# Cross keys by seven block products, exponentials straight from PSUM, and block sums of the gate weights made at loading, in a decoder layer

## The chip, the cores and the metric

The kernel runs on one core of one Trainium2 chip, in float32. A core has five engines that run side by side, each with its own in-order queue: TensorE (matrix products into PSUM; in the profile PE, and PEld for its weight loads), VectorE (DVE), ScalarE (ACT), GpSimd (POOL) and SyncE (SP), from which most DMAs are issued. The metric is device time in microseconds. Before the change the median of three runs is 1415.14 us (1413.28 to 1415.62). The profiled execution took 1413.7 us, of which its span is 1411.5.

## The reference, cut to what matters

The program is one pre-norm decoder layer on 16 sequences of 112 tokens with width 512 and 16 heads of 32: self-attention, cross-attention on a context of 375 rows with a mask, and a gated feed-forward layer with a Walsh-Hadamard transform. What the change touches:

```python
# cross-attention
k = _nan_clean(proj(at, Wk, bk, T))          # 16 batches of 375 context rows
scores = jnp.einsum('bhsd,bhtd->bhst', q, k) / scale
scores = jnp.clip(scores, -50.0, 50.0)
scores = jnp.where(attend, scores, -10000.0)
scores = jnp.clip(scores, -50.0, 50.0)
probs = jax.nn.softmax(scores, axis=-1)
...
# feed-forward
up_gate = jnp.einsum('bsd,hd->bsh', x, W1)
up_lin = jnp.einsum('bsd,hd->bsh', x, W3)
hidden = jax.nn.silu(up_gate) * up_lin
```

A masked score is -50 after the second clip, so its exponential is exp(-50).

## The kernel before, in words

`finite_layer` computes the layer under the assumption that all values are finite and within limits, and collects statistics (`seen`) on the way. Near the end they become one flag, `unfit`; `decoder_layer` reads it and runs the careful `general_layer` if it is set. All times here are of runs without it.

TensorE's order is written out by hand (line 1497, `manual_schedule`): its instructions run in the order of the source. The instructions of the other engines are ordered by a planner, which takes what it expects to be ready, earlier source lines first; `issue_after` holds instructions behind a named one. Each engine then runs its queue in order on the chip.

Stages: self-attention of 16 batches (`lay`, line 1525), cross-attention of 16 batches in three steps each (lines 1572 to 1609), then two feed-forward passes of half the tokens (lines 1636 to 1694).

`Filler` holds generators of independent work. Each `yield` carries a planned cost in microseconds; `fill(us)` draws pieces until that much is spent, with over- or underspending carried on, and `drain` runs the rest. So what TensorE does between two attention steps is fixed by the planned costs. In the cross stage batch `b` is attended while keys, values and queries of `b + 1` are made as filler: with 20.5 us planned for keys and values, 6.0 for queries (made for two batches at every odd `b`), 13.0 for the projection of a finished group of batches at `b` = 0, 4 and 8, and 2.0 for its transposes at `b` = 2, 6 and 10; a third goes to each step.

One cross step (`Cross.step`, line 1128) takes one of three blocks of 125 context rows: 16 score products fill two PSUM tiles `sc` of two banks each; VectorE clips each to SBUF (line 1141), with the upper limit per row from the mask (`hi`); ScalarE takes the exponential in place (line 1144). On TensorE the weighted values of the step before follow (`weigh`, line 921), after a third step its key sums too (line 932), then filler. VectorE adds the exponentials of the three blocks (line 1164) and, in `Pending.store`, takes the reciprocal of the sums (line 951) and multiplies (line 952).

`Keys.keys` runs `features` (line 846): for each of four column groups, four products of 375 columns into one `mm` bank, then an eviction with bias on ScalarE (line 859). There are two `mm` banks, in turn, shared with all filler. `squares` (line 864) has VectorE put the sums of squares of keys and queries into `seen`. `Keys.values` makes value rows per block (line 883; evicted on line 888).

The feed-forward pass computes each pair of 128-column blocks of W1 and of W3 by seven products of half-size blocks (`Pass.products`, line 1337), which needs four sums of weight blocks. They are made in the cross stage, in batches 1 to 9: `weight_sums` (line 1198) loads the raw blocks, adds them on VectorE behind the clip (line 1218), and stores 1 MB tiles to DRAM; `load_blocks` (line 1222) reads these back, one for each of 16 tiles of a pass. All 1 MB weight tiles share eight buffers (tag `w`); normalised tiles and other rows share four (tag `row`).

## Time and profile before

| what | value |
|---|---|
| median of three runs | 1415.14 us |
| profiled execution | 1413.7 us, span 1411.5 us |
| TensorE busy | 1383.3 us (98%) |
| VectorE busy | 790.0 us (56%) |
| ScalarE busy | 365.3 us (26%) |
| cross stage, about 340 to 855 us | TensorE 509.3, VectorE 326.6, ScalarE 162.9 of 515 us |
| DMA | 115.89 MB, mean 82 GB/s |

A row of groups gives line, engine, operation, output<-inputs, shapes and count, then busy time, mean ns of one, and the idle time of the engine just ahead of these instructions with what ended it. A float32 product of the source is two MATMUL records. Busy time of overlapping records is counted once, so a group's busy time divided by its count can be less than its mean. The chain is the work that ended last, followed back; its lines give start, length and line, with the count of instructions.

### The profile page before, as it was taken

The numbers are of one execution on the slowest core, as the hardware profiler recorded it, in microseconds if no ns is written. First come the engines' busy times: TensorE is split into PE (matmuls) and PEld (weight loads), VectorE is DVE, ScalarE is ACT, GpSimd is POOL, SyncE is SP. The second block draws the span as 40 slices with busy tenths as digits, with TensorE's granted clock in tenths as the row PEclk, the third lists the DMA queues.
The fourth block names the chain that finished last, engine by engine and source line by source line (L and its number), as shares of the span: only waits on it lengthen the run. The fifth ranks groups of instructions, "written<-read, shape, count | busy, mean of one in ns | idle before, by whom it ended". The sixth has DMA issues, their size and how long they took to land.

```text
span 1411.5 us, 19018 instructions
## 1 busy us (share of the span) xinstructions
PE 1383.3 (98%) x8096; PEld 764.8 (54%) x8096; DVE 790.0 (56%) x1340; ACT 365.3 (26%) x561; POOL 30.7 (2%) x46
## 2 busy tenths in 40 slices
PE   8999999999999999999999999999999999999997
PEld 5555555556565646564656655554555555555553
DVE  5146987676566586558665547745644224444332
ACT  3245352324133323331333333111110001111000
POOL 2000010101001000000000000000000000000000
PEclk9999999999999999999999999999999999999999
DMA  8100002611123324322020010223022223521301
GB/s 313 47 1 23 8 16 75 243 56 44 38 100 132 113 91 133 112 83 82 23 82 23 23 61 31 92 88 118 30 94 85 90 97 122 191 90 63 116 0 54
DMA packets 49729, 115.89 MB, mean 82 GB/s; under 512 B 2896, under 2 KB 31584, under 8 KB 41188
## 3 DMA queue, kind: packets, MB, share of 16 engines
q1 hardware_dynamic: 47968, 111.39, 22.3%
q0 software_dynamic: 672, 1.62, 0.4%
q10 hardware_dynamic: 996, 1.59, 0.3%
q8 instruction: 65, 1.06, 0.3%
q14 instruction: 28, 0.23, 0.0%
HBM read 86.80 MB, written 27.79 MB: 81 GB/s over the span
## 4 chain that ended last, share of the span: by engine, by line
PE 90%; DVE 6%; DMA 1%; ACT 1%; issue 1%; ACTq 0%; POOLq 0%
PE mm L851 21%; PE mm L883 13%; PE gate L1351 12%; PE mm L894 7%; PE ys L1351 7%; PE gate L1287 6%; PE mm L1351 5%; PE sc L910 4%; PE ys L921 4%; PE ys L1287 3%; PE mm L1287 3%; PE ys L932 2%; PE sc L1017 1%; DMA cT<-in_ctx 1%; PE mm L1435 1%; PE mm L812 1%
## 5 line engine op out<-in xcount | busy, mean ns | idle before, releaser
L883 PE MATMUL mm<-xv,cT 128*125 128x512 f32 x384 | 173.3, 598 | 1.8 <-ACT v L888 1.8
L851 PE MATMUL mm<-cT,xk 128*128 128x375 f32 x512 | 167.5, 483 | 3.5 <-DMA cT<-in_ctx 2.2
L851 PEld LDWEIGHTS mm<-cT,xk 128*128 128x128 f32 x512 | 95.3, 190 | 73.5 <-issue 11.1
L883 PEld LDWEIGHTS mm<-xv,cT 128*125 128x125 f32 x384 | 70.0, 188 | 81.3 <-issue 73.7
L1351 PE MATMUL gate<-t,f 128*128 128x448 f32 x256 | 101.4, 539 | 0.0
L1141 DVE TENSOR_SCALAR e<-sc,hi 125x896 f32<-125x896 f32 x64 | 70.8, 1144 | 48.6 <-PE sc L910 48.6
L951 DVE RECIPROCAL r<-ys 128x448 f32<-128x448 f32 x32 | 94.3, 2947 | 2.8 <-PE ys L932 2.8
L1144 ACT ACTIVATE e<-e 125x896 f32<-125x896 f32 x64 | 60.9, 952 | 115.5 <-DVE e L1141 82.7
L1287 PE MATMUL gate<-h,f 128*128 128x448 f32 x224 | 86.6, 539 | 0.0
L998 DVE TENSOR_REDUCE mx<-sc 112x8 f32<-112x896 f32 x32 | 33.5, 1085 | 87.3 <-PE sc L910 87.3
L1351 PE MATMUL gate<-xyT,f 128*128 128x448 f32 x192 | 80.1, 540 | 0.0
L1351 PE MATMUL ys<-t,f 128*128 128x448 f32 x192 | 77.4, 539 | 0.0
L1351 PEld LDWEIGHTS gate<-t,f 128*128 128x128 f32 x256 | 48.6, 190 | 47.6 <-issue 47.2
L867 DVE CUSTOM_DVE_ANT_0 junk<-kT 128x375 f32<-128x375 f32 x64 | 34.2, 534 | 64.1 <-ACT kT L859 64.1
L1164 DVE TENSOR_TENSOR es<-es,e 125x896 f32<-125x896 f32 x64 | 68.6, 1090 | 0.4
L1141 DVE TENSOR_SCALAR es<-sc,hi 125x896 f32<-125x896 f32 x32 | 36.6, 1147 | 52.1 <-PE sc L910 45.4
L1287 PEld LDWEIGHTS gate<-h,f 128*128 128x128 f32 x224 | 42.5, 190 | 41.3 <-issue 40.9
L888 ACT COPY v<-mm 125x512 f32<-125x512 f32 (+1 forms) x64 | 37.0, 580 | 105.2 <-PE mm L883 105.1
L910 PEld LDWEIGHTS sc<-q,kT 32*125 32x125 f32 x1536 | 46.2, 183 | 31.9 <-issue 19.8
L859 ACT ACTIVATE kT<-mm,bk 128x375 f32<-128x375 f32 x64 | 36.5, 572 | 89.9 <-PE mm L851 89.9
L883 PE MATMUL mm<-wv,xyT 128*112 128x512 f32 x128 | 57.8, 596 | 0.3 <-ACT v L888 0.3
L1367 ACT COPY u<-gate 128x448 f32<-128x448 f32 x16 | 8.5, 532 | 186.2 <-PE gate L1351 163.3
(179 smaller groups left out, 1940.0 us busy)
## 6 DMA issues: line engine op xcount, KB each, us to landing
f<-blocks SPq DMA_DIRECT2D x46, 1024.0 KB, 4.8
blocks<-o SPq DMA_DIRECT2D x16, 1024.0 KB, 5.4
cT<-in_ctx SPq DMA_DIRECT2D x16, 750.0 KB, 4.9
o<-in_f_w SPq DMA_DIRECT2D x32, 256.0 KB, 3.7
w<-in_f_w SPq DMA_DIRECT2D x4, 1024.0 KB, 9.2
blocks<-w SPq DMA_DIRECT2D x4, 1024.0 KB, 6.5
xr<-in_x SPq DMA_DIRECT2D x2, 1024.0 KB, 10.5
out_y<-o SPq DMA_DIRECT2D x8, 256.0 KB, 4.8
```

The lines of the kernel that those rows point to most:

```text
L851: nc.tensor.matmul(acc[:, :n], w[:, c, ts(j, P)], src[:, c, :], start=(c == 0), stop=(c == C - 1))
L883: nc.tensor.matmul(acc[:n, :], src[:, c, :], w[:, c, :], start=(c == 0), stop=(c == C - 1))
L888: nc.scalar.copy(dst[:n].rearrange("p h r -> p (h r)"), acc[:n, :])
L894: nc.tensor.matmul(acc, xyT[:, c, ts(t, P)], w[:, c, :], start=(c == 0), stop=(c == C - 1))
L910: nc.tensor.matmul(views[i // 2][:, i % 2, j, :], k_of(i, j), q_of(i, j), start=True, stop=True)
L921: nc.tensor.matmul(y[ts(i, DH), j, :], v[:, HG * j + i, :], es[i // 2][:n, i % 2, j, :], start=first and j == 0, stop=last, skip_group_che ...
L951: nc.vector.reciprocal(r, sums)
L1141: self.clip = nc.vector.tensor_scalar(e[:KP], sc, -CLIP, hi[:, n : n + 1], op0=ALU.max, op1=ALU.min).ins
L1144: nc.scalar.activation(e[:KP], e[:KP], AF.Exp, scale=SCALE)
L1164: nc.vector.tensor_tensor(total, total, late[3][i][:KP], ALU.add)
L1287: nc.tensor.matmul(banks[m][bank], o[:, c, ts(m, P)], t[:, c, :], start=first and c == 0, stop=c == UNITS - 1, skip_group_check=True,)
L1351: nc.tensor.matmul(bank, o[:, s, k, :], t[:, k, :], start=first and k == 0, stop=k == 1, skip_group_check=True,)
```

## The change

1. **Keys.** `Keys.keys` no longer calls `features`. The 512 x 512 weight and the 512 x 376 context block (a column of zeros is added by a GpSimd memset) are cut into 2 x 2 blocks, and seven products of half-size blocks take the place of eight. Four sums of weight blocks (`xks`) are made once; four sums of context blocks (`t_sums`) for each batch, at the start of the batch before. A product is 4 matmuls of 188 columns into one bank (`a`, `b` and `d`, from the two `mm` buffers); ScalarE evicts bank `a` twice with the bias, VectorE adds the others up into the key tile. Each product yields a planned 1.28 us.
2. **Exponentials.** VectorE's clip goes. ScalarE reads the scores from PSUM with a scale per row (0 for masked rows) and a bias per row (-50 for masked rows). The lower limit is checked by a Relu over the scores, in place in PSUM, with its sum into `low`; the upper limit by a Relu on the reciprocals of the sums, into `top`. Both must be zero in the end, or the flag is set. The reciprocal is taken in two halves. The four ScalarE passes come ahead of the weighted values in the source.
3. **Statistics.** `squares` goes, for keys and queries.
4. **Gate weights.** `weight_sums` and its tiles in DRAM go. `load_blocks` loads the two raw halves and has VectorE make the four sums in the loaded tile.
5. **Order.** The filler takes the first two value blocks, then keys, then the third; keys and values are planned at 19.5 us (from 20.5), the first keys at 9 (from 12.5). The raw mask now uses a `row` buffer.

```diff
+    zero = keep.tile([P, 2 * B * KC + B], F32, name="zero")
+    nc.gpsimd.memset(zero, 0.0)
+    low, top = zero[:, : 2 * B * KC], zero[:, 2 * B * KC :]
...
-    mi = keep.tile([KP, B * KC], I32, name="mi")
+    mi = row("mi").bitcast(I32)[:KP, : B * KC]
     nc.gpsimd.dma_start(out=mi, in_=mask_t)
...
+    nc.gpsimd.tensor_scalar(scl, mi, 0.5, SCALE, op0=ALU.is_gt, op1=ALU.mult)
+    nc.gpsimd.tensor_scalar(nscl, scl, -1.0, None, op0=ALU.mult)
+    nc.gpsimd.tensor_scalar(bia, mi, 0.5, 50.0, op0=ALU.is_gt, op1=ALU.mult)
+    nc.gpsimd.tensor_scalar(bia, bia, -50.0, None, op0=ALU.add)
...
     def store(self):
...
-            nc.vector.reciprocal(r, sums)
+            for c in range(0, C, 2):
+                nc.vector.reciprocal(r[:, ds(c, 2)], sums[:, ds(c, 2)])
+            if over is not None:
+                nc.scalar.activation(
+                    sums, r, AF.Relu, scale=-1.0, bias=limit[:, 1:], accum_out=over
+                )
...
+    def s_sums(s, a11, a12, a21, a22):
+        for k, x0, x1, op in (
+            (0, a21, a22, ALU.add),
+            (1, s[:, 0], a11, ALU.subtract),
+            (2, a11, a21, ALU.subtract),
+            (3, a12, s[:, 1], ALU.subtract),
+        ):
+            nc.vector.tensor_tensor(s[:, k], x0, x1, op)
...
     class Keys:
...
+            nc.gpsimd.memset(self.c[:, :, S2 : 2 * HK], 0.0)
+
+        def sums(self):
...
+            t_sums(self.t, *self.bs)
 
         def keys(self):
             self.k = big("kT")
-            yield from features(self.k, xk, self.c[:, :, :S2], S2, bk)
-            squares(self.k, S2, self.b)
...
+            def product(acc, lhs, rhs, first):
+                for m in range(2):
+                    for k in range(2):
+                        nc.tensor.matmul(
+                            acc[:, m],
+                            lhs[:, k, ts(m, P)],
+                            rhs[:, k],
...
+                return 1.28
...
+            a = bank()
+            took = product(a, a11, b11, True)
+            for m in range(2):
+                nc.scalar.activation(
+                    c21[:, m], a[:, m], AF.Identity, bias=bk[:, 2 + m : 3 + m]
+                )
+            yield took
+            b = bank()
+            took = product(b, s[:, 1], t[:, 1], True)
+            for m in range(2):
+                st(
+                    c12[:, m],
+                    in0=b[:, m],
+                    scalar=dbk[:, m : m + 1],
+                    in1=c21[:, m],
+                    op0=ALU.add,
+                    op1=ALU.add,
+                )
+            yield took
+            took = product(a, a12, b21, False)
+            for m in range(2):
+                nc.scalar.activation(c11[:, m], a[:, m], AF.Identity, bias=bk[:, m : m + 1])
+            yield took
+            took = product(b, s[:, 2], t[:, 2], False)
+            add(c22, b, c21, ALU.add)
+            yield took
+            d = bank()
+            took = product(d, s[:, 0], t[:, 0], True)
+            add(c22, d, c22, ALU.add)
+            yield took
+            took = product(b, a22, t[:, 3], False)
+            add(c21, b, c21, ALU.add)
+            yield took
+            took = product(d, s[:, 3], b22, False)
+            add(c12, d, c12, ALU.add)
+            yield took
...
     def step(self, b, kc, q, keys, f, us):
...
-                self.clip = nc.vector.tensor_scalar(
-                    e[:KP], sc, -CLIP, hi[:, n : n + 1], op0=ALU.max, op1=ALU.min
-                ).ins
-                nc.scalar.activation(e[:KP], e[:KP], AF.Exp, scale=SCALE)
...
+                nc.scalar.activation(
+                    es[i], sc, AF.Exp, scale=scl[:, n : n + 1], bias=bia[:, n : n + 1]
+                )
+            for i, sc in enumerate(scs):
+                nc.scalar.activation(
+                    sc,
+                    sc,
+                    AF.Relu,
+                    scale=nscl[:, n : n + 1],
+                    bias=limit[:KP, :1],
+                    accum_out=low[:KP, 2 * n + i : 2 * n + i + 1],
+                )
+            self.weigh(late)
...
     def load_blocks(u, i):
         o = block_tile("f")
-        nc.sync.dma_start(out=o, in_=blocks[u][i])
+        for half in range(2):
+            nc.sync.dma_start(
+                out=o[:, ds(2 * half, 2)].rearrange("p s k m -> p (s k) m"),
+                in_=f_w[i][:, ts(u + UNITS * half, P)].rearrange("(c p) m -> p c m", p=P),
+            )
+        s_sums(o[:, 4:], *(o[:, k] for k in range(4)))
         return o
...
-    lay(12, 12.5, kv[0].keys())
+    kv[0].sums()
+    lay(12, 9, kv[0].keys())
...
         if b + 1 < B:
-            f.add(kv[b + 1].keys())
-            us += 20.5
+            kv[b + 1].sums()
+            us += 19.5
...
-                f.add(kv[b + 1].values())
+                f.add(kv[b + 1].values(range(2, KC)))
...
-        if 1 <= b <= UNITS + 1:
-            for sums in prepared[-1:]:
-                next(sums)
```

## The prediction

> **What bounds the kernel now.** I read the page first, then the chain in order of time around one cross batch, the windows, the groups by form, and timelines of the cross and feed-forward stages.
>
> ```profile
> PE 1383.3 (98%) x8096; PEld 764.8 (54%) x8096; DVE 790.0 (56%) x1340; ACT 365.3 (26%) x561; POOL 30.7 (2%) x46
> PE 90%; DVE 6%; DMA 1%; ACT 1%; issue 1%; ACTq 0%; POOLq 0%
> ```
>
> TensorE is busy for 98% of the span and carries 90% of the chain, so time is won by giving it less to do, and lost wherever its hand-written order meets a bank that is not yet empty. Windows over the cross stage (340 to 855) and the two gated halves of the feed-forward stage; the columns are length, PE, PEld, DVE, ACT, POOL, clock, DMA share, GB/s:
>
> ```profile
> 340.00:855.00 515.00, 509.32 (x4282) 301.70 (x4280) 326.63 (x564) 162.91 (x236) 5.56 (x5) 1.00 0.22 76
> 895.00:1058.00 163.00, 163.00 (x448) 82.52 (x447) 83.83 (x173) 26.27 (x48) 0.00 (x0) 1.00 0.24 85
> 1143.00:1314.00 171.00, 171.00 (x477) 87.59 (x476) 72.94 (x118) 26.72 (x48) 0.00 (x0) 1.00 0.35 121
> ```
>
> TensorE idles 5.7 us in the cross stage and not at all in the two others. The granted clock is 1.00. One piece of the chain in batch 1 (start, length), and the earlier weight fold from the timeline:
>
> ```profile
> 385.45 1.07 PE sc L910 x32
> 386.52 0.90 PE ys L921 x32
> 387.43 0.75 PE ys L932 x8
> 388.18 10.28 PE mm L851 x32
> ...
> 400.43 6.25 PE mm L851 x32
> ```
> ```profile
> 10.44 3.89 PE L840 MATMUL mm<-bdm,raw_q 128*128 128x128 f32 x32 [0.35 <-ACT bdm L829]
> ```
>
> A product of the source is two MATMUL records. The keys of a batch are 32 records of 375 columns, 0.321 us each; the queries, 32 of 224 columns, 0.195; the fold, 32 of 128 columns, about (3.89 - 0.28)/31 = 0.117, each with its own weights. The groups that the change touches (busy, mean ns, idle before):
>
> ```profile
> L1141 DVE TENSOR_SCALAR e<-sc,hi 125x896 f32<-125x896 f32 x64 | 70.8, 1144 | 48.6 <-PE sc L910 48.6
> L1144 ACT ACTIVATE e<-e 125x896 f32<-125x896 f32 x64 | 60.9, 952 | 115.5 <-DVE e L1141 82.7 <-DVE rstd L771 14.4 <-DVE rstd L772 14.3
> L859 ACT ACTIVATE q<-mm,bq 128x224 f32<-128x224 f32 x32 | 14.2, 443 | 23.0 <-PE mm L851 23.0
> L1218 DVE TENSOR_TENSOR o<-o 128x256 f32<-128x256 f32 x64 | 24.1, 434 | 0.0
> ```
>
> **1. Fewer key products: -16.4 us.** 7 products of 4 matmuls of 188 columns are 56 records instead of 32. Between 128 and 375 columns the rows lie on a line that begins near 10 ns; from 0.195 at 224 with slope (0.321 - 0.195)/151 = 0.00083 us a column, 188 columns cost 0.165. So 56 x 0.165 = 9.26 against 10.28: 1.02 us a batch, 16.4 us in 16. Weight loads show 190 ns apiece; if they set the pace, 56 x 0.190 = 10.64 and the change would lose 0.36 a batch (+5.8), but the fold runs a fresh weight every 0.117, so they overlap.
>
> The Trainium skill (TensorE: Matmul & The Clock Gate, "Back-to-back issue gap") speaks against small products: in a stream of loads and matmuls it gives about 81 ns at 128 columns and 131 at 512, most of it not proportional to the columns. By a line through those figures 188 columns cost 0.785 of 375, and as an estimate from that page the keys would take 14.1 us a batch, +61 us in all. The rows at 128, 224 and 375 in this trace are almost proportional, so I go by them.
>
> **2. The ScalarE queue.** VectorE loses 96 clips (107.4 us), 96 sums of squares and 64 block sums in this stage, and gets per batch four token sums and four sums from PSUM of 376 columns (0.55, between the 434 ns at 256 and the 690 at 512) and two of 188 (0.37). It falls by about 100 of its 327 us and is no candidate. ScalarE gains 96 Relu passes. Exp took 0.951 from SBUF; a copy of the same size from PSUM took 0.906; a bias read per partition adds 0.10 (Identity on 375 columns 0.572, copy interpolated 0.469). With scale and bias as pointers, 0.906 + 0.20 = 1.10, and back to back they start some 0.98 apart (two Exp in a timeline span 1.78). Exp, Exp, Relu, Relu with the accumulator reads (a VectorE one took 0.083) are about 4.3 us from the end of the scores. Lower bound 3.6 (four plain ones overlapped), upper 5.2 (a Relu of 1.4 with its read). All of this now stands ahead of every eviction in the fill of that step, where before ScalarE had two Exp. Stage total: 163, + 101 for the passes, + 14 for pointers on Exp, + 10 for the Relu over sums, - 11 for shorter key evictions, is 277 of some 505 us, so only order matters.
>
> From the planner's costs and the new 19.5 us I worked out which products start each step. Fill begins 0.83 us after the scores, 1.66 with key sums. A product is 1.32 us; its two evictions on ScalarE about 0.72 (0.41 each from the 443 ns at 224 columns, overlapped).
> - Batches 12 and 14, second step: it starts with products 1, 2, 3. Product 3 adds to the bank of product 1, and is ready at 0.83 + 2.64 = 3.47; that bank is read at 4.3 + 0.72 = 5.05. Wait 1.6 x 2 = 3.2 (bounds 1.8 and 5).
> - Batches 0, 8 (third step) and 2, 6, 10 (second): they start with products 2, 3, 4; product 5 takes the bank of product 3, ready at 4.80, read at 5.05. 0.25 x 5 = 1.3 (0 to 6).
> - Batches 4 and odd ones have value rows of 3.44 us first, or products after them: nothing. Odd batches open their first step with eight query halves. The third query column group is ready at 1.66 + 3.12 = 4.78 and needs the eviction of the first (0.44), behind the four. If the second Exp waits for the key sums to release its buffer, or the new Relu over the sums (about 0.65, after the 2.95 us reciprocal) goes first, that is 5.4 or 6.0. Wait 0.1, 0.65 or 1.3 in each of 7; I take 0.4, 2.8 in all (0.7 to 9.1), since the order of ready work usually fills such a gap.
> - Batch 15, with steps of only 5.6 us: scores come back 4.28 after the last ones and need the Relu done: 0.1 (0 to 1).
>
> The skill speaks against this part too (ScalarE: Activation LUTs, "Rules for kernel authors": take VectorE for relu, max and min). The trace shows the clip at 1.14 us on VectorE and about 1.1 estimated for ScalarE, so per pass there is no difference here. By the rule the Relu passes would lie on VectorE, ScalarE would be free at 2.1 us, and by the working above the waits of 3.2 and 1.3 would go: a sum 4.5 us lower.
>
> **3. Waits that go: -2.9.** From the list of TensorE's waits (us, times, longest):
>
> ```profile
> PE ys L932 <- DVE es L1164: 1.6, 2, 1.0
> PE mm L851 <- ACT kT L859: 1.3, 1, 1.3
> ```
>
> The first is for sums of exponentials behind clips, the second for key evictions of the old form. Bounds 0 and -5.7, the whole idle time of the stage.
>
> **4. First keys (self batch 12): +0.8 (0 to 2.2).** The weight sums (4 x 0.69) fit before the context block lands, which TensorE waited for until 285.35. Product 1 needs no sum; product 2 needs two token sums of 0.55 and VectorE is then in the softmax (283.18 to 290). If planned first they are ready at 286.5, in time; if after the two maxima and subtractions, at 288.4, 1.7 late. The memset of the odd column is on POOL, behind the beta additions (over at 276.2 there); later ones have two batches of lead.
>
> **5. Start: +0.5 (0 to 1.9).** The mask is now held in one of four row buffers that the first four normalised tiles also want. POOL read it at 15.39 to 15.98; with three more small operations and three memsets ahead it would be about 17.0, and the fourth tile was written at 15.2. If that tile gets the first tile's buffer (transposed by 15.1) nothing is lost; if the mask's, some 1.9.
>
> **6. Block sums at loading: +1.0 (0 to 31).** Removed: 16 stores and 32 loads of 1 MB. The 32 pairs of raw loads move to the feed-forward stage: 64 issues of 0.50 us on SP, two per 10.5 us tile, landing in 3.7 us as the median. VectorE gets 32 x 4 x 0.434 = 55.6 us, 27.8 in each half: 112 of 163 and 101 of 171. Half the engine idles, but the queue is in order: sums whose load is late hold the additions behind them. A product here is 1.50 us; product 6 must find the third bank added, 3.0 us after it was written. The cover is the lead of four to six buffers.
>
> ```profile
> o<-in_f_w SPq DMA_DIRECT2D x32, 256.0 KB, 3.7
> f<-blocks SPq DMA_DIRECT2D x46, 1024.0 KB, 4.8
> ```
>
> The final check grows by four operations of some 0.2 us off the path: nothing; behind it the next token sums wait under 1 us, still covered by products.
>
> **Sum.** -16.4 + 3.2 + 1.3 + 2.8 + 0.1 - 2.9 + 0.8 + 0.5 + 1.0 = -9.6. The profiled execution took 1413.7 (span 1411.5), 1.4 below the median of 1415.14; so 1404.1 for it and 1405.5 for the median. About 0.2% either way (1412.3 to 1418.0) is what this kernel's runs can tell from no change.
>
> **Rivals.**
> - **A, TensorE is fed all through.** The planner slips evictions between the passes: the waits of part 2 go, -16.4 - 2.9 and a little: 1395 to 1400. For it: VectorE waits on ScalarE little today, and key products come after value rows in most batches. Against: the passes are all ready when the scores end.
> - **B, ScalarE becomes the bound of each step.** All upper bounds of part 2 (5 + 6 + 9.1 + 1) with the start and first keys (1.9 + 2.2): -16.4 - 2.9 + 25.2 + 1 = +6.9 at worst, with three quarters of them +0.6: 1411 to 1422.
> - **C, slower: the block sums block VectorE in the feed-forward stage.** A buffer is free when its tile ends (0). If the sums stand before the additions of the next tile's products 2 and 3 and the load lands at L, the third bank is added at L + 1.74 + 1.24, and product 6 is ready at 7.5: a wait of L - 4.5. With 1.0 for two issues and 3.7 it is 0.2; with the 4.8 of the large loads, 1.3. In the 22 tiles that are not loaded early (32 less six and four), 1.3 is 29 us: 1418 to 1434. It decides from 0.5 a tile, L = 5.0, where 22 waits eat the 9.6. For it: raw loads took up to 11 us. Against: the lead, and sums not planned before the load is expected.
> - **D, weight loads set the pace at 190 ns:** the gain becomes +5.8, 1428; the fold row speaks against it.
>
> **How the numbers follow.** The forecast 0.45 (its own range 1400 to 1411), A 0.19, B 0.16, C 0.17, D 0.03. Faster: forecast and A, and 0.02 of B: 0.66. Same: most of B, 0.12. Slower: C, D and the rest of B: 0.22. The range reaches into A and C: 1396 to 1424.
>
> **What would show it.** Right: L851 gone from the keys, 896 records of 188 columns at 165 ns in the chain; cross stage near 505 us with TensorE idle 8 to 13; feed-forward windows still without idle time; in the wait list, TensorE for the ScalarE key evictions in batches 12 and 14. Wrong: records of 188 columns at 190 ns; TensorE waiting on block sums or additions in the gated halves; a late fourth tile at 17 us; ScalarE passes well over 1.2 us.

## The result: 0.2% slower, and the profile after

The changed kernel takes 1418.34 us as the median of 17 runs (1414.34 to 1420.27), the kernel before on the same chip 1415.14 (17 runs). The ratio is 1.0021, 95% interval 1.0012 to 1.0030. The forecast was 1405.5, faster; the time lies inside the range given (1396 to 1424), on the other side of no change. The profiled execution took 1418.34 us, its span 1416.6.

The page of the changed kernel: busy time by engine, then the chain's shares by engine.

```profile
PE 1372.9 (97%) x8480; PEld 815.2 (58%) x8480; DVE 743.9 (53%) x1315; ACT 475.8 (34%) x785; POOL 33.8 (2%) x68
PE 88%; DVE 6%; ACT 2%; DMA 2%; issue 1%; POOL 0%; SPq 0%; DVEq 0%; ACTq 0%; POOLq 0%
```

TensorE has 10.4 us less to do (1383.3 before), and the span is 5.1 us longer: 15.5 us more idle time. Some of the busy time is work at a lower clock, too. The windows of before, and two more (length, PE, PEld, DVE, ACT, POOL, clock, DMA share, GB/s):

```profile
340.00:855.00 515.00, 503.09 (x4681) 352.21 (x4680) 253.08 (x414) 272.56 (x454) 6.91 (x18) 1.00 0.09 27
895.00:1058.00 163.00, 163.00 (x447) 82.28 (x446) 97.22 (x229) 26.25 (x48) 0.00 (x0) 1.00 0.15 46
1143.00:1314.00 171.00, 171.00 (x476) 87.66 (x475) 85.81 (x166) 26.58 (x48) 0.00 (x0) 1.00 0.23 76
284.00:346.00 62.00, 54.43 (x413) 38.65 (x414) 41.31 (x63) 17.29 (x26) 6.68 (x9) 0.94 0.08 26
848.00:879.00 31.00, 26.34 (x276) 13.72 (x275) 20.31 (x35) 14.88 (x23) 0.00 (x0) 0.89 0.25 69
```

The feed-forward halves are full, as forecast. VectorE is lightly loaded in the cross stage (253 of 515 us) and ScalarE near the forecast 277. The new idle time is dense in two short windows, around the first keys and around the last cross batch, and of these windows they alone have a granted clock under 1.

Where the 5.1 us come from is seen by cutting both timelines of TensorE at the same pieces of work (the ends are the spans as the page rounds them, to 0.1):

| stretch | before | after | difference |
|---|---|---|---|
| start to the first queries | 17.66 | 17.89 | +0.23 |
| to the first key product | 267.69 | 267.77 | +0.08 |
| self batch 12, with the first keys | 14.48 | 21.28 | +6.80 |
| to the first cross scores | 45.83 | 47.49 | +1.66 |
| cross stage, to the first gate product | 526.53 | 524.01 | -2.52 |
| feed-forward stage to the end | 539.31 | 538.16 | -1.15 |

The cross stage, cut at the first scores of each batch (the last row ends at the first gate product), with the runs that are told of below:

| batch | before | after | e2 | e5 | e9 | e10 |
|---|---|---|---|---|---|---|
| 0 | 39.72 | 39.27 | 39.73 | 38.95 | 39.19 | 39.09 |
| 1, 3, 7, 11, 13 (each) | 33.70 | 32.77 | 33.75 (11: 34.26) | 32.78 | 32.78 | 32.77 |
| 2, 10 (each) | 30.72 | 29.31 | 31.03 | 29.31 | 29.31 | 29.31 |
| 4 | 37.95 | 41.53 | 37.95 | 37.18 | 36.97 | 36.97 |
| 5 | 35.93 | 32.77 | 33.75 | 35.39 | 32.78 | 32.77 |
| 6 | 29.46 | 28.83 | 30.53 | 28.82 | 28.82 | 28.82 |
| 8 | 41.38 | 43.45 | 41.38 | 40.61 | 41.70 | 40.89 |
| 9 | 37.11 | 32.78 | 33.75 | 37.48 | 34.60 | 34.59 |
| 12, 14 (each) | 27.65 | 28.05 | 27.65 | 27.06 | 28.05 | 27.06 |
| 15 | 19.75 | 26.80 | 20.98 | 23.39 | 23.85 | 20.84 |

In an undisturbed batch the keys save 0.93 us. Batches 5 and 9 win 2.23 and 3.40 beyond that. Batches 4 and 8 lose 4.51 and 3.00 against it, batches 12 and 14 1.33 each, and batch 15 loses 7.05.

TensorE's waits in the cross stage of the changed kernel, which answer to the list of before (us, times, longest):

```profile
PE mm L1094 <- DVE kT L1115: 6.5, 5, 2.9
PE ys L918 <- DVE xyT L954: 4.7, 1, 4.7
PE mm L1094 <- ACT kT L1108: 2.6, 2, 1.3
PE mm L823 <- ACT v L885: 0.7, 3, 0.2
```

All that the list of before held (`es`, `kT L859`) is gone. The two largest entries are waits for VectorE, although it is busy for less of the window than ScalarE (253 against 273 us). L1115 is the eviction of the second key product (the `st` of `keys`, bank `b`) and L954 the multiplication by the reciprocal in `Pending.store`.

**First keys.** TensorE's timeline of the changed kernel (start, length, line, count; in brackets the idle time before):

```profile
285.66 2.56 PE L1094 MATMUL mm<-cT,xk 128*128 128x188 f32 x8 [2.47 <-DMA cT<-in_ctx]
288.02 2.14 PE L1094 MATMUL mm<-kt,xks 128*128 128x188 f32 x8
289.99 1.44 PE L1094 MATMUL mm<-cT,xk 128*128 128x188 f32 x8
295.76 4.49 PE L1094 MATMUL mm<-kt,xks 128*128 128x188 f32 x16 [4.33 <-DVE kT L1115]
300.09 0.93 PE L1019 MATMUL sc<-ident,e 112*112 112x112 f32 x8
```

and VectorE's of the same stretch:

```profile
286.63 1.13 DVE L1056 TENSOR_TENSOR kt<-cT,kt 128x376 f32<-128x376 f32 x2
287.67 2.08 DVE L1000 TENSOR_REDUCE mx<-sc 112x8 f32<-112x896 f32 x2
289.67 2.08 DVE L1002 TENSOR_TENSOR e<-sc,mx 112x896 f32<-112x896 f32 x2
291.67 2.96 DVE L949 RECIPROCAL r<-ys 128x224 f32<-128x224 f32 x2
294.54 0.31 DVE L1115 SCALAR_TENSOR_TENSOR kT<-mm,dbk,kT 128x188 f32<-128x188 f32 x1
294.77 0.61 DVE L954 SCALAR_TENSOR_TENSOR xyT<-ys,r 128x448 f32<-128x448 f32 x1
295.31 0.40 DVE L1115 SCALAR_TENSOR_TENSOR kT<-mm,dbk,kT 128x188 f32<-128x188 f32 x1
```

Product 2 fills bank `b` at about 290. Its eviction stands in VectorE's queue behind the softmax and two reciprocals, so product 4, which adds to that bank, waits. The products after each of the two waits run at half pace: an undisturbed product takes 1.44 and the next starts 1.28 later; here two took 4.33 us twice, 1.77 too many each time. The first 1.77 only fill part of the wait that follows (see part 4 below).

**Batch 4.** VectorE first, then TensorE, of the changed kernel:

```profile
515.27 1.46 DVE L789 TENSOR_SCALAR xn<-xr,seen,rstd 128x512 f32<-128x512 f32 x3
516.65 0.73 DVE L1115 SCALAR_TENSOR_TENSOR kT<-mm,dbk,kT 128x188 f32<-128x188 f32 x2
517.43 2.23 PE L1094 MATMUL mm<-kt,xks 128*128 128x188 f32 x8 [2.72 <-DVE kT L1115]
```

Product 2 ended at 513.44. Its eviction begins 3.2 us later, when VectorE is through with normalising the finished group (L771 to L789, from 503.56 on, with two additions of exponentials in between).

**Batch 15.** VectorE first, then TensorE, of the changed kernel:

```profile
850.96 1.55 DVE L1046 TENSOR_TENSOR f<-f 128x256 f32<-128x256 f32 x4 [1.55 <-DMA f<-in_f_w]
852.85 1.56 DVE L1046 TENSOR_TENSOR f<-f 128x256 f32<-128x256 f32 x4 [0.33 <-DMA f<-in_f_w]
854.70 1.55 DVE L1046 TENSOR_TENSOR f<-f 128x256 f32<-128x256 f32 x4 [0.30 <-DMA f<-in_f_w]
858.56 1.55 DVE L1046 TENSOR_TENSOR f<-f 128x256 f32<-128x256 f32 x4 [2.30 <-DMA f<-in_f_w]
860.03 2.96 DVE L949 RECIPROCAL r<-ys 128x224 f32<-128x224 f32 x2
863.02 0.62 DVE L954 SCALAR_TENSOR_TENSOR xyT<-ys,r 128x448 f32<-128x448 f32 x1
```
```profile
858.00 1.14 PE L907 MATMUL sc<-q,kT 32*125 32x112 f32 x32
863.80 1.72 PE L918 MATMUL ys<-es,v 125*32 125x112 f32 x32 [4.66 <-DVE xyT L954]
865.45 5.80 PE L891 MATMUL mm<-xo,xyT 128*128 128x512 f32 x8
```

The key sums were done at 854.4; the reciprocal starts at 860.03, since the block sums of four gate tiles stand ahead of it and wait for their loads. Weighing takes 1.72 us instead of 0.97 and a projection 5.80 instead of 3.70.

### The profile page after: what moved, and what is told of

It is laid out like the page before. It is cut to its first block, busy times and chain, and to the rows that moved or that the text cites. A ratio compares the mean times of both kernels' runs of the same rounds, so it can differ in the third digit from the quotient of the medians.

```text
span 1416.6 us, 19994 instructions
## 1 busy us (share of the span) xinstructions
PE 1372.9 (97%) x8480; PEld 815.2 (58%) x8480; DVE 743.9 (53%) x1315; ACT 475.8 (34%) x785; POOL 33.8 (2%) x68
## 4 chain that ended last, share of the span: by engine, by line
PE 88%; DVE 6%; ACT 2%; DMA 2%; issue 1%; POOL 0%; SPq 0%; DVEq 0%; ACTq 0%; POOLq 0%
PE mm L880 14%; PE gate L1429 12%; PE mm L1094 9%; PE mm L862 9%; PE ys L1429 7%; PE mm L891 7%; PE gate L1365 6%; PE mm L1429 5%; PE sc L907 4%; PE ys L1365 3%; PE ys L918 3%; PE mm L1365 3%; PE sc L1019 1%; PE ys L929 1%; DMA cT<-in_ctx 1%; PE mm L823 1%
## 5 line engine op out<-in xcount | busy, mean ns | idle before, releaser
L880 PE MATMUL mm<-xv,cT 128*125 128x512 f32 x384 | 174.2, 598 | 0.0
L949 DVE RECIPROCAL r<-ys 128x224 f32<-128x224 f32 x64 | 94.8, 1522 | 54.7 <-PE ys L929 54.6
L880 PEld LDWEIGHTS mm<-xv,cT 128*125 128x125 f32 x384 | 69.7, 187 | 79.7 <-issue 77.2
L1242 ACT ACTIVATE sc<-sc,limit,nscl 125x896 f32<-125x896 f32 x96 | 102.6, 1069 | 0.0
L1238 ACT ACTIVATE e<-sc,bia,scl 125x896 f32<-125x896 f32 x64 | 68.4, 1094 | 74.1 <-PE sc L907 74.1
L1094 PE MATMUL mm<-kt,xks 128*128 128x188 f32 x384 | 73.0, 338 | 10.9 <-DVE kT L1115 10.9
L1046 DVE TENSOR_TENSOR f<-f 128x256 f32<-128x256 f32 x128 | 49.4, 417 | 47.2 <-DMA f<-in_f_w 46.7
L1094 PEld LDWEIGHTS mm<-kt,xks 128*128 128x128 f32 x384 | 64.4, 197 | 15.2 <-DVE kT L1115 12.6
L880 PE MATMUL mm<-wv,xyT 128*112 128x512 f32 x128 | 57.9, 596 | 0.3 <-ACT v L885 0.3
L1429 PEld LDWEIGHTS ys<-t,f 128*128 128x128 f32 x192 | 36.5, 190 | 35.7 <-issue 35.3
L1429 PEld LDWEIGHTS gate<-xyT,f 128*128 128x128 f32 x192 | 36.0, 190 | 34.4 <-issue 33.5
```

The lines of the kernel that those rows point to most:

```text
L880: nc.tensor.matmul(acc[:n, :], src[:, c, :], w[:, c, :], start=(c == 0), stop=(c == C - 1))
L949: nc.vector.reciprocal(r[:, ds(c, 2)], sums[:, ds(c, 2)])
L1046: nc.vector.tensor_tensor(s[:, k], x0, x1, op)
L1094: nc.tensor.matmul(acc[:, m], lhs[:, k, ts(m, P)], rhs[:, k], start=first and m == 0 and k == 0, stop=k == 1, skip_group_check=True,)
L1238: nc.scalar.activation(es[i], sc, AF.Exp, scale=scl[:, n : n + 1], bias=bia[:, n : n + 1])
L1242: nc.scalar.activation(sc, sc, AF.Relu, scale=nscl[:, n : n + 1], bias=limit[:KP, :1], accum_out=low[:KP, 2 * n + i : 2 * n + i + 1],)
```

## The experiments

Three theories stood at the start. V: TensorE waits at a few places for VectorE's in-order queue, and runs at half clock after. S: the ScalarE passes set each step. K: products of 188 columns don't save what their records promise. Ratios are to the kernel before on the same chip, whose medians lay between 1413.45 and 1414.52; the changed kernel's is 1.0021. Stretches and batches are compared between the profiled executions, one of each kernel.

### e1: block sums held behind the weighing of batch 14

```diff
-            nc.vector.scalar_tensor_tensor(
+            self.last = nc.vector.scalar_tensor_tensor(
                 xyT[:, :, ts(b, S)], in0=y, scalar=scale, in1=r, op0=ALU.mult, op1=ALU.mult
-            )
+            ).ins
+            self.stores.append(self.last)
...
-        s_sums(o[:, 4:], *(o[:, k] for k in range(4)))
+        with tc.issue_after(pending.stores[B + 14]):
+            s_sums(o[:, 4:], *(o[:, k] for k in range(4)))
```

> The block sums of the gate weights are held on VectorE behind the last multiplication of cross batch 14, all else as changed. Theory V (TensorE waits for VectorE's in-order queue at a few places, and its clock is halved for some 4 us after each): in batch 15 the reciprocal no longer stands behind loads, the 4.7 us wait and the slow records after it (0.8 + 2.3) go: -7.8, 1410.5 us. Theory S (the four ScalarE passes set each step): 1418, no change. Theory K (seven products of 188 columns are no less work on the chip than the rows say): 1410 to 1418, says nothing.

Measured: 1412.82 us (ratio 0.9993, 0.9984 to 1.0001); cross stage 516.49, which is 7.5 less: 6.0 in batch 15, and 1.6 in batch 4, where the wait is the same 2.73 us but the clock did not fall after it. Batch 15 takes 20.84, the wait for `xyT` is gone, weighing is 0.97 and projections 3.70 again. What stays against before (19.75) is a wait of 0.4 for the last addition of exponentials and key sums of 1.95. So the block sums do cost time, in batch 15 and nowhere else.

### e2: all keys by sixteen products of 375 columns again, without token sums, all else as changed

```diff
         def sums(self):
+            return
...
         def keys(self):
+            self.k = big("kT")
+            yield from features(self.k, xk, self.c[:, :, :S2], S2, bk)
...
-    lay(12, 9, kv[0].keys())
+    lay(12, 12.5, kv[0].keys())
...
-            us += 19.5
+            us += 20.5
```

> Keys as before (16 matmuls of 375 columns, eviction with bias on ScalarE), planned at 20.5 and 12.5 us as before; exponentials, limits, gate weights and the order of filler as changed; the four weight sums are still made and unused. Theory V: the products' gain of 1.02 us in 16 batches is lost (+16.4), the waits of products for VectorE (4.3 + 2.7 + 2.9 + 0.9) with their slow clock (3.4 + 1.6) and for ScalarE (2.6) and the late context block (1.7) go (-20): about 1414.5. Theory S: the waits move to other evictions, 1418 + 10 = 1428. Theory K: 1402, since the keys would cost more than they save by themselves.

Measured: 1410.35 us (0.9979, 0.9970 to 0.9988). Without the seven products the change is faster than the kernel before. The smaller products save what their records promise in every batch that nothing disturbs (33.75 to 32.77), so K falls; yet in the order given they lose more than that: 6.8 us at the first keys, and batches 4 and 8 go from 37.95 and 41.38 to 41.53 and 43.45. The rest of the change takes 2.2 and 3.4 us off batches 5 and 9.

### e3: the lower limit of the scores is not verified

```diff
-            for i, sc in enumerate(scs):
-                nc.scalar.activation(
-                    sc,
...
-                    accum_out=low[:KP, 2 * n + i : 2 * n + i + 1],
-                )
             self.weigh(late)
```

> The Relu passes over the scores are left out, so the lower limit of the scores is not checked; all else as changed. Theory V: only the two waits of 1.3 us for ScalarE in batches 12 and 14 go, 1415.5. Theory S: ScalarE is free 2.2 us earlier in each of 48 steps, -10 or more, 1408 or less. Theory K: no change, 1418.

Measured: 1416.74 us (1.0017, 1.0008 to 1.0025); cross stage 522.63. The 96 Relu passes are 102.6 us of ScalarE, and taking them away brings 1.4 us, less than the 3.9 of batch 15 alone, where the wait behind the loads happened to be 2.23 us instead of 4.66. Batches 12 and 14 get 1.12 faster each, every odd one up to 13 0.28 slower; why these get slower no run shows. Theory S falls.

### e4: only the first keys by sixteen products

```diff
-    kv[0].sums()
-    lay(12, 9, kv[0].keys())
+    lay(12, 12.5, kv[0].keys8())
```

> Only the first batch's keys (made in self-attention batch 12) by 16 matmuls of 375 columns, planned at 12.5 us as before; all other keys by seven products. Theory V: that stretch takes 14.6 us as before in place of 21.35, -6.8, 1411.5. Theory S: no change, there are no Relu passes in that stretch. Theory K: -1 to 0.

Measured: 1408.60 us (0.9958, 0.9946 to 0.9971). Self batch 12 takes 14.49 instead of 21.28. So at that place the seven products lose 6.8 us, although each batch's keys by themselves save 0.9.

### e5: projections of the finished group behind the keys, and batches 12 and 14 filled earlier

```diff
         if bl == 0:
-            if g == 0:
-                f.add(after_self(whole[3], n2[3]))
-            elif g < 3:
-                f.add(AfterCross(whole[g - 1], n3[g - 1]).pieces())
             us += 13.0 if g < 3 else 0.0
...
             f.add(kv[b + 1].values(range(2)), kv[b + 1].keys())
+            if bl == 0:
+                if g == 0:
+                    f.add(after_self(whole[3], n2[3]))
+                elif g < 3:
+                    f.add(AfterCross(whole[g - 1], n3[g - 1]).pieces())
+            if g == 3:
+                us += 2.0 * (b % 2 == 0)
```

> The changed kernel with two changes of order: at the start of each group of four batches the output projections of the group before (and the normalising on VectorE behind them) come after the key products instead of before them, and batches 12 and 14 get 2 us more fill in each step, so that key product 1 is done one step earlier. Theory V (TensorE waits on VectorE's queue at a few places, and runs at half clock after): the waits at product 4 of batches 4 and 8 (2.72 and 2.9 us) go, with the slow records behind the first (1.7), and the two ScalarE waits of 1.3: cross scores to first gate 524.0 minus 9.9, 514.1 us, and about 1408.5 in all against 1418.3. Theory S (the ScalarE passes set each step): the two waits of 1.3 alone go, 1415.7. If the normalising only meets the next queue in the same way one step later: no change, 1418.

Measured: 1412.88 us (0.9996, 0.9986 to 1.0007); cross stage 518.44, of which 3.4 less in batch 15 is only a shorter wait behind the loads (2.25 us instead of 4.66) with fewer slow records after it. Batches 4 and 8 fall by 4.35 and 2.84 and batches 12 and 14 by 1.0 each, as theory V has it; but batches 5 and 9 rise by 2.62 and 4.70. The wait moved. ScalarE in batch 5 of the next run, which has the same order, shows the new one:

```profile
521.69 0.45 ACT L870 ACTIVATE q<-mm,bq 128x224 f32<-128x224 f32 x1
522.44 0.45 ACT L870 ACTIVATE q<-mm,bq 128x224 f32<-128x224 f32 x1 [0.30 <-PE mm L862]
526.76 0.64 ACT L952 ACTIVATE ys<-r,limit 128x448 f32<-128x448 f32 x1 [3.87 <-DVE seen L764]
527.43 0.76 ACT L870 ACTIVATE q<-mm,bq 128x224 f32<-128x224 f32 x2
```

L952 is the new Relu over the reciprocals. The reciprocal stands on VectorE behind the normalising of the finished group (until 526.7), so the Relu waits, and the query evictions behind it on ScalarE wait too; TensorE then lacks a bank (2.4 us, "PE mm L880 <- ACT q L870"). One late VectorE instruction held up two queues.

### e6: all places mended

Held block sums (e1), plain first keys (e4), the order of e5, and the token sums of batch 1 behind the last self-attention softmax:

```diff
+            if b == 0:
+                with tc.issue_after(last_self):
+                    kv[1].sums()
```

> Keys of 188 columns from batch 1 on, first keys by 16 products of 375, the feed-forward block sums held behind the weighing of cross batch 14, the order of the previous run, and the token sums of batch 1 held behind the softmax of the last self-attention batch. Theory V: the gains add: start 17.8, queries to keys 267.3, first keys 14.5, to the cross scores 46.2, cross stage 524.0 - 7.5 - 9.9 = 506.6, feed-forward 538.3: a span of 1390.7 and a time of 1392.5, 1.6% below the kernel before. Theory K (the smaller key products save little of the 16.4 us that the records promise): not under 1400.

Measured: 1402.17 us (0.9922, 0.9908 to 0.9935): faster than both kernels, and 9.7 us over what was expected. The stretch to the cross scores is 45.84 (47.66 in e4, which has the same first keys), so the token sums of batch 1 had cost 1.8 us there: in the changed kernel they stood ahead of the softmax and waited for their context block until 340.4. The cross stage is 516.21 instead of 506.6; 7.7 us of that are batches 5 and 9 (35.46 and 37.78), and 1.6 were expected twice: the slow records of batch 4 are in the 7.5 taken from e1 and in the 9.9 expected of e5.

### e7: TensorE kept busy in the gap of batch 15, first form

```diff
+            if b == B - 1 and kc == 1:
+                for _ in range(32):
+                    nc.tensor.matmul(
+                        wide[0][:, 1, 448:], ident, ident[:, :64], start=True, stop=True,
...
             self.weigh(late)
```

> The changed kernel with 32 products of 128 x 64 of the identity (about 4.1 us by the records of 128 columns, halved), written to unused columns of a scores bank and read by nobody, between the scores and the weighing of batch 15, where TensorE idled 4.66 us. The wait for VectorE stays as long as it was; TensorE is only kept busy in it. If the slow records behind the wait are the clock's answer to idle time: the weighing takes 0.97 again instead of 1.72 and the projection 3.7 instead of 5.8, cross scores to first gate 524.0 - 2.9 = 521.1 and about 1415.4 in all. If they are slow because of the block loads that run at that time, or of the memory, they stay at 1.72 and 5.8 and the time at 1418.

Measured: 1432.59 us (1.0134, 1.0118 to 1.0149). The test missed its aim: the products waited 5.73 us themselves, for the Relu over the same scores tile, and then took 13.92 us instead of about 4. The windows of this run show one reason why the records were slow, the clock:

```profile
858.00:865.00 7.00, 1.33 (x33) 0.96 (x32) 5.20 (x7) 3.80 (x7) 0.00 (x0) 0.81 0.00 0
865.00:872.00 7.00, 6.94 (x33) 6.94 (x33) 0.00 (x0) 1.09 (x3) 0.00 (x0) 0.50 0.00 0
872.00:879.00 7.00, 7.00 (x37) 6.88 (x40) 0.00 (x0) 0.00 (x0) 0.00 (x0) 0.50 0.00 0
879.00:885.00 6.00, 6.00 (x40) 3.17 (x40) 2.09 (x2) 0.00 (x0) 0.00 (x0) 0.68 0.01 3
```

The granted clock stayed at 0.50 for the whole 13.9 us of 64-column products, with no load running, and rose only under the larger ones after. Half a clock makes at most 8 us of the expected 4, so records of 64 columns are also not half as long as those of 128, which the estimate had taken for granted; what they take at full clock no run shows.

### e8: block sums on GpSimd, all else as e6 without the hold

```diff
+        s_sums(o[:, 4:], *(o[:, k] for k in range(4)), nc.gpsimd)
```

> As the run with all places mended, but the block sums of the feed-forward weights are made on GpSimd at loading instead of being held on VectorE. Theory V: VectorE's queue is free of them, so batch 15 loses nothing: 1392 to 1395, and the gated windows without idle time. If GpSimd's sums of 128x256 are slow (over 2.5 us each, four sums and two issues of loads per tile of 10.5 us), the tiles come late and the gated halves get waits: 1400 or more.

Measured: 1407.71 us (0.9952, 0.9938 to 0.9965). Batch 15 takes 19.23, the best of all. The 128 sums take 757 ns each on GpSimd (417 on VectorE), and the feed-forward stage is 543.68, 5.5 longer; TensorE waits 2.1 us there for VectorE (L1460) and runs at 0.57 of its clock in the 2 us after. What of the rest lies in GpSimd's sums and what in that clock is not settled. Holding on VectorE is the better of the two.

### e9: the normalising of a finished group behind the weighing of the next batch

```diff
-                f.add(AfterCross(whole[g - 1], n3[g - 1]).pieces())
+                left = AfterCross(whole[g - 1], n3[g - 1])
+                f.add(left.projections())
...
+        if bl == 1 and 0 < g < 3:
+            f.add(left.later())
...
+        def later(self):
+            with tc.issue_after(pending.stores[-1]):
+                self.finish()
+            yield 0.0
```

> The changed kernel with one part moved: the residual sum and normalising behind the output projections of a finished group (two chains of small VectorE operations, about 10 us) are issued behind the weighing of the first batch of the next group, not as soon as the projections allow. The projections stay where they are. Theory V: product 4 of batches 4 and 8 no longer waits for VectorE, the reciprocal of those batches is not held up either, and nothing else meets the chain: from scores to scores batch 4 takes 37.2 instead of 41.5 us and batch 8 40.6 instead of 43.5, batches 5 and 9 stay at 32.8, cross scores to first gate 524.0 - 7.2 = 516.8, about 1411 in all. Rival: the chain holds up what comes next wherever it is put (in the run with the new order it held up the reciprocal, and 2.7 and 4.7 us came back in batches 5 and 9): no change, 1418.

Measured: 1412.38 us (0.9989, 0.9980 to 0.9998); cross stage 516.52. Batch 4 falls from 41.53 to 36.97 and batch 5 stays at 32.78, as theory V has it. Batch 8 falls by 1.75 only, and 1.82 come back in batch 9, where product 4 waits 1.55 for the same eviction: with four tiles instead of three the chain is longer. Of the 7.5 us, 2.95 are batch 15, which this edit doesn't touch: a shorter wait behind the loads (2.91 us instead of 4.66) and fewer slow records after it.

### e10: e6 with the normalising moved, and the projections left in place

> The run with all places mended (1402.2), with the normalising issued behind the weighing of the next batch, in place of the projections moved behind the keys. Theory V: the 2.7 and 5.0 us that batches 5 and 9 lost there go, batches 4 and 8 stay at 37.2 and 40.6: cross stage 516.2 - 7.7 = 508.5 and 1394.5 us, 1.4% below the kernel before. Rival (the chain always holds up something): 1402.

Measured: 1399.47 us, ratio 0.9899 (0.9884 to 0.9914): 1.0% below the kernel before, and the best version found. TensorE's waits in its cross stage:

```profile
PE mm L1103 <- DVE kT L1124: 3.1, 6, 1.6
PE ys L918 <- ACT eT L1026: 0.7, 1, 0.7
PE mm L823 <- ACT v L885: 0.7, 3, 0.2
PE ys L929 <- DVE es L1282: 0.4, 1, 0.4
```

It is 5 us over what was expected: 1.8 in batch 9, and 2.8 at the first keys, where the wait for the context block happened to be 2.81 us, and the granted clock was 0.50 in the 2 us after it.

### e11: the busy gap again

```diff
+            if b == B - 1 and kc == 1:
+                idle = psum("mm", [P, D])
+                for c in range(C):
+                    nc.tensor.matmul(idle, ident, xo[:, c, :], start=c == 0, stop=c == C - 1)
             self.weigh(late)
```

> The busy gap of batch 15 once more: the products read by nobody now go to a product bank that nobody waits to read, and are 4 of 128 x 512 (8 records, 3.7 us by the rows of the projections), so that they start as soon as the scores end. The wait for VectorE stays. If the slow records behind it are the clock's answer to idle time: weighing 0.97 instead of 1.72 and projection 3.7 instead of 5.8; cross scores to first gate 524.0 - 2.9 = 521.1, about 1415.4 in all. If the block loads or the memory slow them: they stay, 1418.

TensorE's timeline of this run:

```profile
860.56 1.14 PE L907 MATMUL sc<-q,kT 32*125 32x112 f32 x32
861.63 3.70 PE L1253 MATMUL mm<-xo,ident 128*128 128x512 f32 x8
865.26 0.97 PE L918 MATMUL ys<-es,v 125*32 125x112 f32 x32
866.17 3.70 PE L891 MATMUL mm<-xo,xyT 128*128 128x512 f32 x8
```

Measured: 1415.25 us (1.0007, 0.9998 to 1.0017), batch 15 at 22.85 instead of 26.80. With 3.7 us of useless work in the gap, weighing takes 0.97 and the projection 3.70. From the start of the weighing to the next scores the two take 4.54 us; in the changed kernel, from 863.80 to 871.18, 7.38. The remaining 1.1 us of batch 15 are a shorter wait: the multiplication that weighing needs ended at 864.90 here, so the gap would have been about 3.3 us instead of 4.66. Unfilled gaps of 2.23 to 2.91 us at this place lowered the clock in all four runs that have them (0.50 to 0.64 in e3, e4, e5 and e9), and in the changed kernel itself it was 0.50 from 863.80 to 865.80 with a DMA share of 0.00. So the slow records were the clock's answer to idle time, not the loads.

## Why the prediction was wrong, point by point

The forecast's sum and what the stretches and batches show in its place:

| term | forecast | measured |
|---|---|---|
| 1, keys, fifteen batches of the cross stage | -15.4 | -13.95 |
| 2, waits for ScalarE in batches 12, 14 | +3.2 | +2.7 |
| 2, waits for ScalarE in 0, 2, 6, 8, 10 and odd batches | +4.1 | 0 (batches 0, 2, 6, 10: -0.2) |
| 3, waits that go | -2.9 | -5.6 |
| not in the sum: batches 4 and 8 | 0 | +7.5 |
| 6 (and 0.1 of part 2), block sums and batch 15 | +1.1 | +7.05 in batch 15, -1.15 in the feed-forward stage |
| 4, first keys with their own saving of 1.0 | -0.2 | +6.8 |
| not in the sum: token sums of batch 1 | 0 | +1.7 |
| 5, start | +0.5 | +0.3 |

**Right.** Part 1's mechanism and nearly its size: in the chain, records of 188 columns ran at 4.02 us for 24 and 5.09 for 32, 0.1675 and 0.159 each against the forecast 0.165. Rival D (190 ns) is out. The prediction's estimate from the spacing that the Trainium skill states (TensorE: Matmul & The Clock Gate, "Back-to-back issue gap"), a loss of 61 us, does not hold here either. The forms on ScalarE were priced well: Exp from PSUM with pointers 1.095 (1.10 forecast), Relu 1.069 plus 0.20 for its read. The groups:

```profile
L1242 ACT ACTIVATE sc<-sc,limit,nscl 125x896 f32<-125x896 f32 x96 | 102.6, 1069 | 0.0
L1238 ACT ACTIVATE e<-sc,bia,scl 125x896 f32<-125x896 f32 x64 | 68.4, 1094 | 74.1 <-PE sc L907 74.1
```

Batches 12 and 14 wait for ScalarE as worked out, 1.3 each of 1.6. Part 3 was too small: the wait for `es` in batch 5 was followed by key sums of 2.02 instead of 0.94 us, and batches 5 and 9 won 5.6, its far bound.

**Wrong: VectorE "falls by about 100 of its 327 us and is no candidate" (part 2).** The load did fall (by 74 us, to 253 in the window), and VectorE became what TensorE waits for most. The step looked at how full the engine is; what decides is what stands ahead in its queue at the moment when a bank must come free. Before, no filler product of keys needed VectorE. Now product 4 of every batch does, and where a chain of normalising (L771 to L789) or a softmax stands ahead, it waits: 2.72 and 2.9 us in batches 4 and 8. Part 2 gave batch 4 nothing and batch 8 a quarter of a microsecond, because it followed the ScalarE queue alone. e2 and e9 show it: without the seven products, or with the chain moved, batch 4 takes 37.95 and 36.97.

**Wrong: part 4, +0.8 (0 to 2.2).** It asked when the token sums of product 2 would be ready; they were, and product 2 waited for nothing. It did not go on to product 2's eviction, which had the same softmax ahead of it and two reciprocals besides. Product 4 begins 10.10 us after product 1 in all seven profiles with these first keys, whatever the clock. Where the clock was full, 5.66 of that are idle (e1, e3, e5, e7, e9); in the changed kernel 4.33 are, because slow records fill the rest. After this wait the clock takes 1.77 more.

**Wrong: part 6, +1.0, and the place in rival C.** The sentence "sums whose load is late hold the additions behind them" was right as a mechanism; but it was followed through the feed-forward stage only, where VectorE's waits for these loads (most of 46.7 us) cost nothing. The first five tiles are loaded earlier. Four of them land in batch 15, whose steps are the shortest of all, and there the sums held the reciprocal. e1 shows 6.0 us of it. The lead was smaller than part 6 took it for, too, because the key sums `kt` and the weight sums `xks` now take buffers of the tag `w`. In the changed kernel the loads of one gate tile are issued at 818.80, those of three together from 847.0 on, when the last key products of batch 14 release their buffers, and those of a fifth at 851.7. In e2, without the tiles `kt`, two gate tiles are loaded from 717.4 and one from 796.6, and with the same block sums batch 15 takes only 20.98. That run changes the filler as well, so how much of it is the lead is not separated.

**Missing: the price of an idle gap.** Every wait was priced at its own length. The records behind four of them ran slow: by 1.77 us twice at the first keys, 1.77 in batch 4 (517.43 to 521.55, 2.35 in an undisturbed step) and 2.85 in batch 15. The first 1.77 fell into a wait and cost nothing; the others add up to 6.4 us. Without these the profiled execution would be at about 1412 by this sum, faster than before, so the sign of the result hangs on them. e11 shows the cause for batch 15. For batch 4, e1 has the same wait at a clock of 1.00 and is 1.57 us faster, and e4 has it at 0.50 and takes 42.74, 2.78 more than e1. At the first keys only the granted clock speaks for it (0.59 and 0.63 in the 2 us after the gaps). The Trainium skill has a rule that bears on this and that the prediction did not weigh: "TensorE: Matmul & The Clock Gate", in the table of "Why this matters for your kernels", asks for no idle gaps over about 3 us, since a window of idle time takes the clock back to half. The traces agree in kind, with a lower bound: 2.47 us were enough in the changed kernel, 1.79 in e9.

**Rivals.** B (ScalarE as the bound of each step) held the measured time in its range, by luck: e3 rules it out. A's time was reached by e10, 1399.5, once little stood ahead of the evictions. C had the right engine and the wrong stage.

## What to carry to other kernels

When a bank's eviction moves to another engine, list what stands ahead of it in that engine's queue at every place where the product runs; a half-empty engine in strict order is no less late than a full one. Follow the consequence to the next use of the same bank, not only to the first operand. And price a wait on TensorE with the clock behind it: here gaps from 1.8 us on could cost up to about their own length again, and the place for late-loading work is behind what TensorE waits for.

## What the runs showed of the hardware

- **The gap and the clock.** Over the idle gaps of TensorE of more than 1.2 us in the thirteen profiles (from 20 us on), with the granted clock of the 2 us after: up to 1.69 us (19 gaps) it was always 1.00; from 1.79 to 3.24 us (37 gaps) it was 1.00 in 16 and 0.50 to 0.88 in 21; from 4.05 us (9 gaps) 0.50 to 0.63. Gaps of 2.73 us at the same place of the program went both ways (1.00 in e1, 0.50 in e4). The clock records of the traces show where this spread comes from. In each profile all slow stretches begin on one grid of 3.41 us, and those before the end of the program last 3.41, 6.83 or (once, in e7) 20.48 us; in the changed kernel they begin at 286.02, 296.26, 518.13 and 862.88, which is 3, 65 and 101 steps of 3.413 us apart. What counts is how much of a gap lies in one cell of that grid: at most 1.69 us in 30 gaps, none of which lowered the clock; 1.72 to 1.86 in 8, of which 3 did; 1.87 or more in 27, which all did. The gap of 2.73 us had 1.63 in one cell in e1 and 2.24 in e4. So about half a cell of idle time is enough, and a gap of some 1.8 to 3.2 us lowers the clock or not by where it falls on the grid. The Trainium skill (TensorE: Matmul & The Clock Gate, Part 1, "What's actually happening") says that the window of about 3.4 us which is looked at runs freely; the traces agree.
- **A clock that stayed low under work.** In e7 the clock was at 0.50 when 64 records of 64 columns began, back to back, and it stayed there for all of their 13.92 us, with PE and PEld busy; no other slow stretch before the end of a program is longer than 6.83 us. In e11, 8 records of 512 columns began at 1.00 and kept it. Whether the number of columns is the reason is not shown by these two runs.
- **GpSimd's sums.** 757 ns for 128x256 from SBUF to SBUF, against 417 on VectorE.
